# Attention layer of a four-layer graph network: where its value steps, its second softmax and its table loads stand in the order of work

## The chip, the cores and the metric

The kernel runs on one core of one Trainium2 chip. The metric is the device time of one execution in microseconds. The engines are named as the profile names them: PE is TensorE (PEld its weight loads), DVE is VectorE, ACT is ScalarE, POOL is GpSimd, SP is SyncE. [...]

## The reference, cut to what matters

`x` holds 128 graphs of 64 nodes with 256 features each. The kernel keeps it as 64 tiles of 128 partitions (the nodes of two graphs) by 256 features. Four graph layers follow one another, each as a residual with a layer normalisation:

```python
x = _layernorm(x + _L0_gnn_ref(...))   # windows of an LSTM
x = _layernorm(x + _L1_gnn_ref(...))   # two maps with batch norms
x = _layernorm(x + _L2_gnn_ref(...))   # attention over 512 edges
x = _layernorm(x + _L3_gnn_ref(...))   # a spectral layer
```

The change lies in layer 2 and in how layers 1 and 3 meet it:

```python
def _L2_gnn_ref(H, W_lin, W_val, a, W_out, A0, src, dst):
    Xq = (H @ W_lin.T).reshape(bt, n, h, dh)
    Xv = (H @ W_val.T).reshape(bt, n, h, dh)
    e = einsum('behd,hd->beh', leaky_relu(Xq[:, src] + Xq[:, dst], 0.2), a)
    e_t = (e + log(A0[src, dst] + EPS)[None, :, None]).transpose(1, 0, 2)
    ex = exp(e_t - segment_max(e_t, src)[src])
    attn = ex / segment_sum(ex, src)[src]
    Y = segment_sum(attn[..., None] * Vt, src)      # Vt: Xv at dst
    return Y.reshape(bt, n, d) @ W_out.T

def _L3_gnn_ref(features, A, W1, b1, W2, b2):
    # U: eigenvectors of the normalised Laplacian of A
    agg = einsum('mn,bnd->bmd', U.T, features)
    h = relu(agg @ W1 + b1)
    return einsum('nm,bmd->bnd', U, h @ W2 + b2)
```

## The kernel before, in words

**Residual and normalisation.** `X` stays in SBUF through all layers. `Norm` (L1337) adds a product to two tiles of it (`join`, DVE, L1353), takes their statistics (L1362, L1363), and for every n tiles runs one root chain (`inv_sqrt`: DVE L1272, ACT's sqrt L1274, DVE L1275 to L1278, then `ln_sh` L1378) and scales each tile (`X` on ACT, L1383). The root chain and the scaling together are a flush.

**Layer 1's last pass** (`last_pass`, L2048) turns the finished map of layer 1 back, two tiles h at a time, joins them to X and normalises them. `whole(h)` does this for one pair with its own flush; from the pair after that the steps of layer 2 do it themselves.

**Scores** (`scores`, L2227) is a generator of 32 steps, one for two tiles. `follow` (L2145) fixes the order on an engine by hand, and all that it issues is recorded at L2148. Step k expands the products of step k-1 and k to edges (`edges`: 64x512 products `m<-edge_s,xl` and `xh`, whose positive part goes to `xs` on ACT and on DVE), multiplies the next two tiles by both weights (`maps`: `m<-wqv,xT`; the value half is stored to DRAM as `xv`, L2224, from SP's queue except four steps from ACT's), transposes the tiles after these (`transposed`: `m<-ident,X`, then the `xT` copy on DVE) and sums the scores (`products`: `sc<-xs,az`). POOL multiplies `xq` by the attention vector (L2219); DVE sums it, and at the end of each half (16 steps) a linear term `linb` is added to the scores. In the first half of the steps the two pairs `ha` and `hb` of layer 1 are turned and joined as well. Their statistics and the root chain stand partly behind the join (`ha`) and partly in `closed` (`hb`), which runs in the step after; the very last root chain has a place of its own (L2294 to L2296).

**Softmax** (`softmax`, L2303) is a generator of six steps for each half of the scores: shift, exp (L2322), transposes (L2329), sums, a division, and eight indirect DMAs on POOL's queue that scatter the attention values to a DRAM table `attn_d` (L2353). `fetch` (L2358) loads the table of one half back, 4 MB in eight transfers, issued alternately from SP's and POOL's queue, into `M2`.

**Values** (`values`, L2396) is a generator of 33 steps. Step k copies one slice of the table (`load`, `mc` on ACT, L2370), loads `xr` from DRAM (`mapped`, L2376, issued from POOL's queue except four steps from ACT's), multiplies them in 64x64 products (`mixed`, L2390), and copies the result to `yT` (ACT, L2393). It then multiplies the `yT` of step k-1 by the output weights (`ps<-wo,yT`, L2413; called W here) and adds that to tiles 2(k-1) and 2(k-1)+1 of X, with a flush for every four tiles, that is in every second step. Steps 0 to 15 need the first table, steps 16 to 31 the second.

**Layer 3** (`blocks`, L2514) is a generator of 19 steps over 16 blocks of four tiles. Step q does `basis(q)` (products `ps<-bda,X`, L2479, copied to `ag` by ACT, L2481, after which POOL adds `cb` to X, L2483), `first_map(q-1)` (L2489, `h` on DVE, L2492), `back(q-2)` (L2497, `uh` on ACT, L2499) and `second_map(q-3)` (L2507, joined, normalised and stored by SP).

**The order of all this** is written out by hand with `run(...)`, which takes one step of each generator named (L2421 to L2529); within it, a scheduler may still put independent instructions of different steps in another order. Before the change it runs: scores beside layer 1, then scores beside the first softmax, `fetch(0)`, three score steps, seven times a score step and a value step (L2460), and in the last stage the second softmax beside four value steps, then values and layer-3 steps mixed, `fetch(1)`, eight times [value, value, layer 3], two values and the rest of layer 3. There, `basis(q)` for q from 6 on stands behind value step 2q+4.

Of the kernel before, what the change touches and what calls it, by code (L numbers as in the profile page):

```python
# [16 lines left out]
N = 64  # L17
# [4 lines left out]
NT = NB * N // P  # L22
# [1369 lines left out]
def tile_adj_resnorm(ctx: ExitStack, tc: tile.TileContext, I: dict, out: bass.AP, layers: int = 4):  # L1392
    nc = tc.nc
# [653 lines left out]

    def last_pass():  # L2048

        ln = Norm(nc, sy, X, 8, act=True)  # L2050

        def normed(h):
            y = sy.tile([P, 2, 2 * P], F32, tag="y", name="y")
            for c in range(2):
                s.activation(y[:, c, :], Y[h // 2][:, c, h % 2 * 2 * P : (h % 2 + 1) * 2 * P], AF.Identity,
                             bias=sh2[:, c : c + 1], scale=sc2[:, c : c + 1])
            return y

        y = {}

        def turned(h):

            ps, x = pp.tile([P, 512], F32, tag="m", name="m"), y.pop(h)
            for i in range(2):
                for c in range(2):
                    te.transpose(ps[:, i * D + c * P : i * D + (c + 1) * P], x[:, c, i * P : (i + 1) * P], ident)
            ln.join(2 * h, ps, 2)

        def prepare(h):

            if h < 2 * NQ:
                with in_order(s, True):
                    y[h] = normed(h)

        def whole(h):

            with in_order(v, True):
                turned(h)
                ln.stats(2 * h, 2)
            if h == 1:  # L2080
                keep_awake(pp.tile([P, 512], F32, tag="m", name="m"), 2)
            prepare(h + 1)
            with in_order(s, True), in_order(v, True):
                ln.flush()

        prepare(0)
        return ln, turned, prepare, whole
# [10 lines left out]
    with ExitStack() as l2:  # L2098
# [93 lines left out]
        def maps(k, xT, apart=False):  # L2192

            xq, whole, xv = [], sx.tile([P, 2, D], F32, tag="xq", name="xq", bufs=2), sx.tile([P, 2, D], F32, tag="xv", name="xv", bufs=2)
            pss = [pp.tile([P, 512], F32, tag="m", name="m") for _ in range(2)]

            def product(i, cols):
                for c in range(2):
                    follow(te.matmul, pss[i][:, cols], xT[:, i, c, :], wqv[:, c, cols], start=(c == 0), stop=(c == 1))

            def first(i):
                lo, hi = (parts[i][q][:, :: k % 2 + 1][:, :2] for q in range(2))
                x = pss[i][:, :D].rearrange("p (c d) -> p c d", c=2)
                w = whole[:, i, :].rearrange("p (c d) -> p c d", c=2)
                follow(s.copy, hi, x, eng=s)
                follow(s.copy, w, x, eng=s)
                follow(v.tensor_tensor, lo, w, hi.bitcast(F32), ALU.subtract, eng=v)
                xq.append((lo, hi))

            if apart:  # L2210
                for i in range(2):
                    product(i, slice(0, D))
                    first(i)
            for i in range(2):
                product(i, slice(D, 2 * D) if apart else slice(0, 2 * D))
                if not apart:
                    first(i)
                follow(s.copy, xv[:, i, :], pss[i][:, D:], eng=s)
                nc.gpsimd.tensor_tensor(whole[:, i, :], whole[:, i, :], arow, ALU.mult)  # L2219
                yield  # L2220
            sums.append(lambda: follow(
                v.tensor_reduce, lin[:, k // HU, :, :, :, k % HU].rearrange("p c i h -> p i c h"),
                whole.rearrange("p i (c h d) -> p i c h d", c=2, h=2), AX.X, ALU.add, eng=v))
            (s if 22 < k < 27 else nc.sync).dma_start(xvd[k], xv)  # L2224
            yield xq

        def scores():  # L2227


            K = NT // 2  # L2230
            xT = transposed(0)
            *_, xq = maps(0, xT, True)
            whole(2)
            xT = transposed(1)

            def scales(n):

                with in_order(s, True):
                    while n and later:
                        later.pop(0)()  # L2240
                        n -= 1

            held = {}

            def edges(k, c, xq):
                xs, ready = {}, []
                for i in range(2):
                    pl = [pp.tile([P, 512], F32, tag="m", name="m") for _ in range(2)]
                    for part, b in ((0, 0), (0, 1), (1, 0), (1, 1)):
                        r = slice(b * N, (b + 1) * N)  # L2250
                        follow(te.matmul, pl[b], xq[i][part][r, c, :], GGr[r, :], start=(part == 0), stop=(part == 1))
                    for b in range(2):
                        x = xs[b, i] = sx.tile([P, E], F32, tag="xs", name="xs", bufs=8)
                        ready.append(follow(v.tensor_scalar, x, pl[b], 0.0, None, ALU.max, eng=v) if b
                                     else follow(s.activation, x, pl[b], AF.Relu, eng=s))
                held[k, c] = xs, ready

            def closed(n):
                with in_order(v, True):
                    if n:  # L2260
                        ln.stats(2 * n, 2)
                    with in_order(s, True):
                        later.extend(ln.root())

            xl, last = None, None
            for k in range(K):
                ha, hb = (h if h < 2 * NQ else None for h in (2 * k + 3, 2 * k + 4))
                if k:
                    edges(k - 1, 1, xl)
                edges(k, 0, xq)  # L2270
                if hb:
                    prepare(hb)
                if last:
                    closed(last)
                steps = maps(k + 1, xT) if k < K - 1 else iter((None,) * 3)
                next(steps)
                while sums:
                    sums.pop()()
                scales(2)
                next(steps)  # L2280
                scales(2)
                xl, xq = xq, next(steps)
                if k < K - 2:
                    xT = transposed(k + 2)
                if ha:
                    with in_order(v, True), in_order(te, True):
                        turned(ha)
                        if hb:
                            turned(hb)
                        ln.stats(2 * ha, 2)  # L2290
                products([(k - 1, 1), (k, 0)] if k else [(k, 0)], held)
                if hb:
                    prepare(hb + 1)
                elif ha:  # L2294
                    closed(None)
                    scales(2)  # L2296
                last = hb
                if k == K - 1:
                    edges(k, 1, xl)
                    products([(k, 1)], held)  # L2300
                yield

        def softmax(half):  # L2303
# [40 lines left out]
            for c, (eT, rc) in enumerate(zip(eTs, rcs)):  # L2344
                ps = scratch()
                for k in range(4):
# [1 line left out]
                v.tensor_tensor(at[:, :, :, :, c, :].rearrange("p k b u i -> p (k b) i u"),  # L2348
                                eT.rearrange("p k (i u) -> p k i u", u=HU).rearrange("p k (b i) u -> p (k b) i u", b=2),
                                ps.rearrange("p (k i u) -> p k i u", i=4, u=HU), ALU.mult)  # L2350
            for k in range(4):
                for b in range(2):
                    nc.gpsimd.indirect_dma_start(  # L2353
                        out=attn_d[b][:, :], out_offset=bass.IndirectOffsetOnAxis(ap=ix[:, k : k + 1], axis=0),
                        in_=at[:, k, b].rearrange("p u c i -> p (u c i)"), in_offset=None)
# [2 lines left out]
        def fetch(half):  # L2358

            M2[half] = lw.tile([P, N, P], F32, tag="M2", name="M2")  # L2360
            for n0 in range(0, N, 16):
                for b in range(2):
                    (nc.sync, nc.gpsimd)[b].dma_start(
                        M2[half][b * N : (b + 1) * N, n0 : n0 + 16, :],
                        attn_d[b][: N * N, :].rearrange("(d n) q -> d n q", n=N)[:, n0 : n0 + 16, :])

        def load(k):
            half, u_ = divmod(k, HU)
# [6 lines left out]

        def mapped(k):  # L2376
            x = sm.tile([P, 2, D], F32, tag="xr", name="xr", bufs=3)
            (s if 14 < k < 19 else nc.gpsimd).dma_start(x, xvd[k])
            return x

        def mixed(m, x):
# [41 lines left out]
        sc_ = scores()  # L2423
        ln, turned, prepare, whole = last_pass()
        whole(0)
        whole(1)
        run(*[sc_] * (NQ - 1))
        keep1.close()
        lw, sm = own1(valuing, name="l2w", bufs=1), own1(valuing, name="l2s", bufs=2)
# [24 lines left out]
        soft += [softmax(h) for h in range(2)]  # L2454
        run(*[sc_] * (HU - NQ + 1))
        run(*[sc_, soft[0]] * 6)
        fetch(0)
        run(*[sc_] * 3)
        constants()
        run(*[sc_, val] * 7)  # L2460
        scoring.close()
        pp = own1(l2, name="l2m", bufs=2, space=PSUM)

# [3 lines left out]
        with tc.tile_pool(name="l3s", bufs=2) as s3, tc.tile_pool(name="l3p", bufs=6, space=PSUM) as p3:  # L2467
# [55 lines left out]

            l3 = blocks()
            sf = soft[1]
            run(sf, val, sf, val, sf, val, sf, val, sf, l3, l3, val, l3, val)
            fetch(1)
            run(l3, val, l3, val, l3)
            run(*[val, val, l3] * 8, val, val, *[l3] * (NT // 4))  # L2529
        valuing.close()  # L2530


# [60 lines left out]
```

## Time and profile before

| | us |
|---|---|
| three runs, lowest, median, highest | 2227.99, 2230.44, 2233.7 |
| the profiled execution | 2228.17 |
| its span in the profile | 2226.4 |
| busy in the span: PE, DVE, ACT, POOL | 2156.3, 1781.5, 891.8, 206.3 |

The span is the time from the first to the last instruction that the profiler saw, and 1.8 us of the execution lie outside it. PE is busy for 97% of the span; what it misses lies mostly in the last quarter. The page's 40 slices of the span are 55.7 us each; a busy share there says how full an engine is and not what it waits for, so the prediction goes by the waits of PE and by its timeline, and takes durations of single instructions from the groups by form. Two things are to be kept in mind with those rows. A row of the timeline joins neighbouring matmuls of one kind, so its duration is that of the group. And an engine's idle time is put down to the releaser that came last; in brackets behind a row stand the idle time before it and that releaser.

The stages of the span that concern the change are, on PE: layer 1's end at about 1675 us, the scores from there to about 2025 us, and then the last stage.

### The profile page before, as it was taken

The numbers are of one execution on the slowest core, as the hardware profiler recorded it, in microseconds if no ns is written. First come the engines' busy times: TensorE is split into PE (matmuls) and PEld (weight loads), VectorE is DVE, ScalarE is ACT, GpSimd is POOL, SyncE is SP. The second block draws the span as 40 slices with busy tenths as digits, with TensorE's granted clock in tenths as the row PEclk, the third lists the DMA queues.
The fourth block names the chain that finished last, engine by engine and source line by source line (L and its number), as shares of the span: only waits on it lengthen the run. The fifth ranks groups of instructions, "written<-read, shape, count | busy, mean of one in ns | idle before, by whom it ended". The sixth has DMA issues, their size and how long they took to land. (4 is left out here: it accounts for less than half of the span.)

```text
span 2226.4 us, 30062 instructions
## 1 busy us (share of the span) xinstructions
PE 2156.3 (97%) x8828; PEld 1227.0 (55%) x8828; DVE 1781.5 (80%) x9261; ACT 891.8 (40%) x1663; POOL 206.3 (9%) x256
## 2 busy tenths in 40 slices
PE   8999999999999999999999999999998999989897
PEld 6545665445665445665444654554434544447787
DVE  5788887888898899889899899887957886546688
ACT  1432322433332333332333222434436874446575
POOL 0111111101000000000000000000001111313321
PEclk9999999999999999999999999999999999999999
DMA  7001010111010111010111000012210010411522
GB/s 236 22 20 38 1 39 1 38 38 58 1 39 1 39 38 57 1 39 1 38 39 57 1 20 19 8 66 95 76 58 20 29 52 29 114 39 52 144 85 78
DMA packets 44923, 101.55 MB, mean 46 GB/s; under 512 B 5296, under 2 KB 23856, under 8 KB 43472
## 3 DMA queue, kind: packets, MB, share of 16 engines
q1 hardware_dynamic: 37808, 83.59, 10.8%
q0 software_dynamic: 3664, 13.35, 2.2%
q10 hardware_dynamic: 3280, 2.64, 0.5%
q8 instruction: 70, 1.15, 0.2%
q14 instruction: 101, 0.83, 0.1%
HBM read 67.97 MB, written 31.59 MB: 45 GB/s over the span
## 5 line engine op out<-in xcount | busy, mean ns | idle before, releaser
L1756 PE MATMUL pq<-H,wi 128*128 128x512 f32 (+1 forms) x1952 | 780.6, 540 | 1.5 <-ACT gate L1796 1.2
L1796 ACT ACTIVATE gate<-pq,bl 128x512 f32<-128x512 f32 (+1 forms) x504 | 315.5, 632 | 615.0 <-PE pq L1772 501.0
L1756 PEld LDWEIGHTS pq<-H,wi 128*128 128x128 f32 x1952 | 365.5, 190 | 336.8 <-issue 269.7
L1772 PE MATMUL pq<-lh,wh 128*128 128x512 f32 (+1 forms) x1152 | 461.2, 528 | 0.8 <-DVE lh L1814 0.7
L1772 PEld LDWEIGHTS pq<-lh,wh 128*128 128x128 f32 x1152 | 218.4, 190 | 202.4 <-issue 143.5
L1799 ACT ACTIVATE gate<-lc 128x512 f32<-128x512 f32 (+1 forms) x144 | 83.6, 580 | 278.2 <-DVE lc L1811 103.1
L2148 PE MATMUL m<-wqv,xT 128*128 128x512 f32 (+1 forms) x264 | 126.6, 626 | 4.5 <-DVE xT L2148 4.5
L803 POOL PARTITION_ALL_REDUCE qQ<-qSG x62 | 73.8, 1191 | 508.6 <-DVE pc L135 263.6
L2028 PE MATMUL ps<-h,w 128*128 128x512 f32 x256 | 114.5, 604 | 5.0 <-ACT h L2022 2.7
L1383 ACT ACTIVATE X<-X,ln_sh,ln_rs 128x256 f32<-128x256 f32 x187 | 99.1, 593 | 38.8 <-DVE ln_sh L1378 32.4
L1974 PE MATMUL ps<-at,w 128*128 128x512 f32 x256 | 113.1, 593 | 0.0
L2148 DVE TENSOR_SCALAR xs<-m 128x512 f32<-128x512 f32 x128 | 79.6, 677 | 18.5 <-PE m L2148 18.5
L2148 PEld LDWEIGHTS m<-wqv,xT 128*128 128x128 f32 x264 | 51.1, 204 | 66.4 <-issue 49.6
L2148 ACT ACTIVATE xs<-m 128x512 f32<-128x512 f32 x128 | 68.7, 598 | 44.3 <-PE m L2148 43.5
L2028 PEld LDWEIGHTS ps<-h,w 128*128 128x128 f32 x256 | 48.3, 192 | 65.0 <-issue 55.1
L2219 POOL TENSOR_TENSOR xq<-xq,arow 128x256 f32<-128x256 f32 x64 | 46.8, 732 | 377.3 <-DVE xl L2148 377.2
L2148 PE MATMUL m<-edge_s,xl 64*128 64x512 f32 x256 | 68.4, 449 | 13.3 <-ACT xs L2148 11.8
L1974 PEld LDWEIGHTS ps<-at,w 128*128 128x128 f32 x256 | 47.3, 190 | 52.8 <-issue 51.4
L1362 DVE BATCH_NORM_STATS2 ln_st<-X 128x6 f32<-128x256 f32 x192 | 72.9, 415 | 1.3
L2148 DVE TENSOR_TENSOR xl<-xq,xh 128x256 fp32r<-128x256 f32 x64 | 27.3, 426 | 56.6 <-ACT xq L2148 56.6
L131 DVE SCALAR_TENSOR_TENSOR CS<-GA,qE 64x1 f32<-64x1 f32 x294 | 61.8, 210 | 9.5
L131 DVE SCALAR_TENSOR_TENSOR GA<-qtg,CS,GA 64x1 f32<-64x1 f32 x294 | 61.6, 209 | 8.4
(647 smaller groups left out, 3557.5 us busy)
## 6 DMA issues: line engine op xcount, KB each, us to landing
wi<-in_WihT_dram SPq DMA_DIRECT2D x16, 1024.0 KB, 4.9
wh<-in_WhhT_dram SPq DMA_DIRECT2D x12, 1024.0 KB, 6.4
xd<-X SPq DMA_DIRECT2D x16, 512.0 KB, 2.6
X<-xd SPq DMA_DIRECT2D x16, 512.0 KB, 3.4
X<-in_x_dram SPq DMA_DIRECT2D x15, 512.0 KB, 9.0
out_dram<-X SPq DMA_DIRECT2D x15, 512.0 KB, 2.9
xv<-xv SPq DMA_DIRECT2D x28, 256.0 KB, 2.0
xr<-xv POOLq DMA_DIRECT2D x28, 256.0 KB, 2.9
```

The costliest lines, as they stand in the source:

```text
L131: self.nc.vector.scalar_tensor_tensor(o, a, s, b, op0, op1)
L803: gp.partition_all_reduce(S[:, : wide + n], PR[:, : wide + n], N, bass_isa.ReduceOp.add)
L1362: nc.vector.bn_stats(st, self.X[:, k, :])
L1383: nc.scalar.activation(x, x, AF.Identity, bias=sh[:, k : k + 1], scale=rs[:, k : k + 1])
L1756: te.matmul(ps, wi[:, kk, o * P : (o + 1) * P], at(kk, k), start=(kk == 0), stop=(k == 0 and kk == 1))
L1772: te.matmul(ahead[gt, c], wh[:, kk, o * P : (o + 1) * P], hst[:, kk, :M], start=False, stop=(kk == 1))
L1796: s.activation(gates[gt][:, c, :M], ps, AF.Tanh if gt == 2 else AF.Sigmoid, bias=bl[:, p - 1, o : o + 1])
L1799: s.activation(*due.pop())
L1974: te.matmul(ps, w1[:, k, c * P : (c + 1) * P], at[:, k, :], start=(k == 0), stop=(k == 1))
L2028: te.matmul(ys[c], w2[:, k, c * P : (c + 1) * P], h[:, k, :], start=(k == 2), stop=(k == 1))
L2148: ins = make(*a, **k)
L2219: nc.gpsimd.tensor_tensor(whole[:, i, :], whole[:, i, :], arow, ALU.mult)
```

## The change

It does the following:

- Layer 1's last pass takes its small tiles from another pool. `whole` gets a callback that is run behind the join and the statistics and ahead of the flush; `whole(1)` and `whole(2)` use it for the `transposed` of tiles 0 and 1, and `whole(1)` moves into `scores`.
- In `scores` the statistics of both pairs go to `closed` in the step after. The last root chain takes this way too.
- No value step stands beside scores any more: eight score steps follow where seven pairs of a score and a value step stood.
- `fetch` becomes a generator of two portions (the two halves of the partitions, four transfers each), all issued from POOL's queue; the first table's portions alternate with score steps. The scatter runs over the halves first.
- All stores of `xv` and all loads of `xr` are issued from SP's queue.
- The last stage begins with five pairs of a value step and a step of the second softmax, then both portions of the second table. Value and layer-3 steps are then mixed so that `basis(q)` for q from 7 to 15 stands directly behind value step 2q+2.

The number of value steps (33), layer-3 steps (19) and matmuls of each kind stays as it was.

```diff
-        ln = Norm(nc, sy, X, 8, act=True)
+        ln = Norm(nc, sx, X, 8, act=True)
...
-        def whole(h):
+        def whole(h, then=lambda: None):
             with in_order(v, True):
                 turned(h)
                 ln.stats(2 * h, 2)
+            x = then()
             if h == 1:
                 keep_awake(pp.tile([P, 512], F32, tag="m", name="m"), 2)
             prepare(h + 1)
             with in_order(s, True), in_order(v, True):
                 ln.flush()
+            return x
...
-            (s if 22 < k < 27 else nc.sync).dma_start(xvd[k], xv)
+            nc.sync.dma_start(xvd[k], xv)
...
-            xT = transposed(0)
+            xT = whole(1, lambda: transposed(0))
             *_, xq = maps(0, xT, True)
-            whole(2)
-            xT = transposed(1)
+            xT = whole(2, lambda: transposed(1))
...
-            def closed(n):
+            def closed(hs):
                 with in_order(v, True):
-                    if n:
-                        ln.stats(2 * n, 2)
+                    for h in hs:
+                        ln.stats(2 * h, 2)
...
-                        ln.stats(2 * ha, 2)
                 products([(k - 1, 1), (k, 0)] if k else [(k, 0)], held)
                 if hb:
                     prepare(hb + 1)
-                elif ha:
-                    closed(None)
-                    scales(2)
-                last = hb
+                last = [h for h in (ha, hb) if h]
...
-            for k in range(4):
-                for b in range(2):
+            for b in range(2):
+                for k in range(4):
...
-            for n0 in range(0, N, 16):
-                for b in range(2):
-                    (nc.sync, nc.gpsimd)[b].dma_start(
+            for b in range(2):
+                for n0 in range(0, N, 16):
+                    nc.gpsimd.dma_start(
...
+                yield
...
-            (s if 14 < k < 19 else nc.gpsimd).dma_start(x, xvd[k])
+            nc.sync.dma_start(x, xvd[k])
...
-        whole(1)
         run(*[sc_] * (NQ - 1))
...
-        fetch(0)
-        run(*[sc_] * 3)
+        table = fetch(0)
+        run(sc_, table, sc_, table)
         constants()
-        run(*[sc_, val] * 7)
+        run(*[sc_] * 8)
...
-            run(sf, val, sf, val, sf, val, sf, val, sf, l3, l3, val, l3, val)
-            fetch(1)
-            run(l3, val, l3, val, l3)
-            run(*[val, val, l3] * 8, val, val, *[l3] * (NT // 4))
+            run(*[val, sf] * 5)
+            for _ in fetch(1):
+                pass
+            run(val, val, *[l3, val] * 2, *[l3, val, val] * 3, l3)
+            run(*[l3, val, val] * 9, *[l3] * 4)
```

More of the change, by code (lines that the diff above doesn't have):

```diff
@@ L2256, in edges @@
                 held[k, c] = xs, ready
-            def closed(n):
+            def closed(hs):
                 with in_order(v, True):
-                    if n:
-                        ln.stats(2 * n, 2)
+                    for h in hs:
+                        ln.stats(2 * h, 2)
                     with in_order(s, True):
                         later.extend(ln.root())
-            xl, last = None, None
+            xl, last = None, []
             for k in range(K):
```

## The prediction, made before the changed kernel was run

> **What bounds the kernel now.** I read the page's slices first. The tenths of PE are full until the last ten slices (one is 55.7 us), so the change (which touches only the stretch from about 1660 us on) can win only PE's gaps there.
>
> ```profile
> PE   8999999999999999999999999999998999989897
> ```
>
> Then the stretch views. One stretch (1937.4 to 2007.5) holds the scores with value steps between them, the next the steady part of the last stage, the third that stage's start. Columns: length, busy PE, PEld, DVE, ACT, POOL, then PE's clock and the DMA share.
>
> ```profile
> 1937.40:2007.50 70.10, 58.67 (x408) 31.08 (x408) 30.77 (x71) 35.80 (x78) 9.96 (x15) 0.90 0.12 39
> 2101.00:2200.00 99.00, 99.00 (x1034) 88.62 (x1033) 80.70 (x276) 71.43 (x154) 30.96 (x48) 1.00 0.25 80
> 2080.00:2101.00 21.00, 13.12 (x110) 10.53 (x109) 9.63 (x43) 12.61 (x27) 1.14 (x2) 0.76 0.43 123
> ```
>
> The steady part is PE alone: 99.00 of 99.00 us at full clock. The two others lose 11.4 and 7.9 us in waits and more to a clock of 0.90 and 0.76. PE's waits from 1660 us to the end name them:
>
> ```profile
> PE m L2148 <- ACT xs L2148: 11.8, 3, 4.2
> PE ps L2413 <- ACT ag L2481: 5.1, 1, 5.1
> PE m L2148 <- DVE xT L2148: 4.5, 2, 2.3
> PE m L2390 <- ACT mc L2370: 3.0, 1, 3.0
> PE m L2390 <- ACT yT L2393: 2.8, 1, 2.8
> ```
>
> PE's timeline shows what follows a wait (start, duration, idle time before in brackets):
>
> ```profile
> 1837.69 0.50 PE L2148 MATMUL m<-edge_s,xl 64*128 64x512 f32 x2 [3.31 <-ACT xs L2148]
> ...
> 1838.36 5.40 PE L2148 MATMUL m<-wqv,xT 128*128 128x512 f32 x8
> ```
>
> Those 8 products take 3.70 us elsewhere (1914.29). After idle times of 2.2 us and more (2.19, 2.25, 3.31, 4.24, 5.07) PE runs at half rate for some 3.7 us and so loses about 1.85 us; after 1.06, 1.20, 1.61 and 1.69 us it doesn't. [...]
>
> **The change part by part.** Everything is reckoned against the profiled execution: span 2226.4 us, time 2228.17, so 1.8 us outside the span. That execution is 0.1% below the median of the runs (2230.44).
>
> *Start of layer 2.* The xT copy no longer stands behind a root chain on DVE: one wait of 2.25 us and its slow products (1.7) go, while the keep-awake matmuls now stand between. Bounds 0 and 5; I take 3, nearer the sum of 3.9.
>
> *Statistics moved into closed().* A score step with layer-1 normalisation takes 9.47 us (1804.61 to 1814.09), a pure one 8.13 (1912.08 to 1920.21, PE busy throughout). The 1.3 us between them come from a closed loop of DVE and ACT (xs, statistics, root, X, xh, xq, xl, xT, joins). Moving 0.75+0.30 us inside a loop changes its order, not its sum: 0. Bounds: a gain of 7 (half of a join and its aggregations, 0.69+0.30, in each of 15 steps) to a loss of 3 (one instruction of 0.2 us more in each).
>
> *Last root chain.* It goes through an ordinary step instead of standing ahead of the edges: 3.31 + 1.7 = 5.0 gained.
>
> *No value steps beside scores.* Gone: 2.99 and 2 x 4.24 us of waits, 1.4 for the 64x64 matmuls ahead, 3.4 for two slow clocks, 1.3 for three stretched edge groups: 17.6. As a check, 70.1 us of stretch hold 51.9 us at steady durations: 18.2. I take 17.6. The seven value steps' own PE work (2.73 us each: 16 matmul groups 0.90, W 1.83) only moves to the last stage. One thing comes back: after the last score product nothing fills PE between the linear term and the last sc product. Waits of 1.61 and 1.20 become one of about 3.2 with a slow clock: -2.0.
>
> *Table in portions, POOL's queue alone.* xr moves to SP's queue, so POOL's now holds xq's multiplications, scatters, table loads and X+cb. Fetch(0) is needed only some 80 us later (4 MB took about 20 us, 1917.3 to 1939.2). Behind it POOL's xq multiplications feed only the linear term, which is due late. Fetch(1) is issued before the stage's sixth value step and needed at the sixteenth (its first mc): ten value steps (27 us) and seven layer-3 steps of 1.8 to 6.3 us (35) later, some 60 us, against eight scatters of 1.27 us and 20 us of loading: hidden. Cover gone, it would cost what it costs now. The stall of before, whose chain of waits holds the load of M<-attn_d, goes: 5.07 + 1.79 slow + 2.81 + 1.64 slow = 11.3. xv on SP: the xr tile has three buffers and two steps of lead; 0.
>
> Sum of gains: 3 + 0 + 5 + 17.6 - 2 + 11.3 = 34.9.
>
> *The new order of the last stage.* This is the cost. Value step k adds the output of step k-1 to tiles 2(k-1) and 2(k-1)+1 and normalises four tiles in every second step. Layer-3 step q reads tiles 4q to 4q+3 in its first matmuls (basis), so it needs value step 2q+2. Before, step q stood behind value step 2q+4: a whole block (two values, one layer-3 step) lay between. After, from q=7 to q=15, it stands directly behind value step 2q+2. On PE the order of a block is: second_map, W, W, two groups of mixing matmuls, then basis, whose four pairs each wait for ACT's X; then first_map, back. Behind the waiting basis stand, in order, first_map, back, the next second_map and the next W, hence everything.
>
> The chain, with t=0 at second_map's start, and steady durations:
> PE: second_map 0 to 1.83, W to 3.66, W to 5.49, mixing to 7.29.
> DVE: four joins with statistics (0.69 + 0.75 + 0.30), layer 3's root interposed: the last join starts about 5.8; the four layer-2 tiles' is_t is done at 8.9.
> ACT: yT 6.1 to 6.9, mc (1.08) to 7.9, layer 3's X (four, 2.08) 8.45 to 10.5, then the sqrt for layer 2 (0.2), mc to 11.75, and X for layer 2 from 11.75. The first is there at about 12.35.
>
> So PE waits 12.35 - 7.29 = 5.06 us. After such a wait it runs at half rate (1.85 lost, as at 2088.06 below).
>
> ```profile
> 2088.06 3.78 PE L2413 MATMUL ps<-wo,yT 128*128 128x256 f32 x8 [5.07 <-ACT ag L2481]
> ```
>
> These 8 products take 1.99 us in the steady part. The block takes 11.85 us now:
>
> ```profile
> 2134.57 1.95 PE L2479 MATMUL ps<-bda,X 128*128 128x128 f32 x16
> 2136.36 1.95 PE L2489 MATMUL ps<-w,ag 128*128 128x128 f32 x16
> 2138.14 1.06 PE L2497 MATMUL ps<-bdah,h 128*128 128x128 f32 x8
> 2139.03 1.89 PE L2507 MATMUL ps<-w,uh 128*128 128x256 f32 x8
> ...
> 2146.42 0.83 PE L2479 MATMUL ps<-bda,X 128*128 128x128 f32 x6
> ```
>
> It becomes 11.85 + 5.06 + 1.85 = 18.76: 6.91 more. Seven blocks (q=7 to 13): 48.4. At q=14 one mixing group stands before the basis, so 0.90 less of the wait is covered (7.8), at q=15 none (8.7). Sum 64.9.
>
> Its bounds. Below: with empty engines the chain from the end of W to the first X is join, statistics, root and X: 3.19 us from join to X (1965.08 to 1968.27) plus 0.2 and the first X 0.59, together 4.0; mixing covers 1.8, so PE still waits 2.2, 20 us in nine steps, or 22.5 with the longer last two. Without the half rate the middle is 48. Above: everything as worked out.
>
> Net: 34.9 - 64.9 = -30.0. Span 2226.4 + 30.0 = 2256.4, time **2258 us**, 1.3% slower.
>
> **Rivals.**
>
> *The new wait is near its bare length* (2.2 us, the clock not always halved): 34.9 - 22.5 = +12.4, time 2216. For it: DVE and ACT have gaps in the steady part (80.7 and 71.4 of 99 us), and the waits let both run ahead. Against it: ACT's queue in a block puts layer 3's four X and a mc between the value tiles' sqrt and their X. If even this is hidden the gain stands whole: 2193.3. The point that decides is the cost of a block: below 34.9/9 = 3.9 us the kernel becomes faster. 0.17 together.
>
> *Waits as worked out, but no half rate*: 48 instead of 64.9, time 2242. For it: the 64x64 matmuls after the wait of 2.99 were not visibly slower. Against it: the five waits from 2.2 us up, listed above. 0.2.
>
> *The second table is late in spite of its early issue.* It stands on POOL's queue behind scatters and the first X+cb, which needs layer 3's first basis; were it to slip to the seventeenth value step, the 11.3 us come back with the wait: 2269. For it: eight loads stand on one queue where two served before; against it: some 30 us to spare by the sum above. 0.06.
>
> *The change does not do what it says*: the score steps stay at 70 us for 52 us of work because something other than the value steps stalled them. ACT's mc, yT and X do lie between xs in the trace, so it is unlikely: 17.6 less gain, 2276. 0.04.
>
> *Values alone are bound by ACT*: at the start of the last stage five value steps run beside the softmax: ACT needs 0.65 + 1.08 + 1.15 = 2.88 a step against PE's 2.73. A few us, inside the range.
>
> **How the numbers follow.** The forecast 0.5 (2248 to 2266), no half rate 0.2, short waits 0.17, late table 0.06, no gain in scores 0.04, the rest (mixes near no change) 0.03. The range leaves out the short waits and the very end: 2222 to 2276. A difference below 0.3%, 6.7 us, can't be told from none. Faster by more: 0.17. Within: 0.09, from blocks that cost 3.1 to 4.6 us ((34.9 -/+ 6.7)/9), a mix of bare waits and slow clocks. Slower: 0.74.
>
> **What would show it.** In the waits of PE a row of basis (ps) on ACT's X, nine times or, by X tile, more, some 5 us each; PE's clock some 0.8 to 0.9 in the last 170 us instead of 1.00, and blocks of 18.7 us instead of 11.85. The scores end some 20 us earlier for their work, with no wait of 4.24 on xs. No wait of PE on mc, ag or yT near the table. Wrong would be: a basis that waits below 3 us, or a scheduling in which layer 3's X come after those of layer 2; a gain below 25 us ahead of the last blocks; or waits of 5 us with the clock at 1.00.

## The result, and the profile after

| | us |
|---|---|
| before, median (4 runs) | 2229.53 |
| after, median (4 runs, 2259.8 to 2265.01) | 2263.11 |
| ratio after / before | 1.0146 (1.0127 to 1.0165) |
| predicted time and range | 2258.0 (2222 to 2276) |
| after, profiled execution and its span | 2259.8, 2258.0 |

The changed kernel is 1.5% slower. PE's waits from 1660 us to the end, after the change (us in total, times, longest):

```profile
PE ps L2476 <- ACT X L1383: 32.2, 9, 6.0
PE m L2150 <- ACT X L1383: 5.3, 2, 3.4
PE m L2388 <- ACT yT L2391: 4.8, 8, 2.3
PE sc L2150 <- DVE xs L2150: 4.3, 2, 3.2
PE m L2388 <- ACT mc L2368: 3.4, 1, 3.4
...
PE m L2388 <- issue: 2.0, 3, 1.1
```

The first row is new and the largest: basis waits for ACT's X nine times, 32.2 us in all. What led the list before has gone or shrunk: xs on ACT from 11.8 to 0.9 us, xT from 4.5 to 0.2, and ag (5.1) is gone. The other rows are where something else took a place: the transposes at the start of layer 2 now wait for ACT's X (5.3 us, 2.5 before), the mixing waits for yT (4.8 us, 2.8 before, in one piece then), the score steps run out with one wait of 3.2 us, and the first slices of the second table are waited for once.

Five of the late blocks, in the stretch view (length, PE, PEld, DVE, ACT, POOL, clock, DMA share, GB/s):

```profile
2102.40:2192.10 89.70, 68.54 (x641) 62.67 (x641) 40.52 (x165) 46.20 (x96) 14.47 (x20) 0.87 0.18 56
```

Where this stage had PE busy for 99.00 of 99.00 us at a clock of 1.00, PE now misses a quarter of the stretch, and its clock is 0.87. DVE and ACT are below 52%, so no engine is full: they wait for one another. One block on PE's timeline shows how:

```profile
2126.28 1.89 PE L2504 MATMUL ps<-w,uh 128*128 128x256 f32 x8
2128.01 3.62 PE L2411 MATMUL ps<-wo,yT 128*128 128x256 f32 x16
2131.56 0.98 PE L2388 MATMUL m<-mc,xr 64*64 64x64 f32 x32
2132.76 0.97 PE L2388 MATMUL m<-mc,xr 64*64 64x64 f32 x32 [0.23 <-ACT yT L2391]
2137.73 1.22 PE L2476 MATMUL ps<-bda,X 128*128 128x128 f32 x4 [3.99 <-ACT X L1383]
...
2139.17 2.25 PE L2476 MATMUL ps<-bda,X 128*128 128x128 f32 x12
```

It is the order of the prediction: second_map, W, W, mixing, mixing, and then a basis that waits 3.99 us. The two rows of basis hold 16 records in 1.22 + 2.25 us, where the steady part before took 1.95: the half clock (granted 0.59 of full speed from 2137.73 to 2141.42, and 0.50 behind the next such wait, from 2155.17 to 2159.40; 1.00 in the steady part). From basis to basis it is 17.65 us (2120.08 to 2137.73) where it was 11.85; five blocks (2102.44 to 2192.07) take 17.93 on average. Not all nine basis steps wait like this: the waits are 0.29 and 0.77 us at q=7 and q=8, 3.99 or 4.00 at q=9 to 13, then 5.12 and 6.03. At q=7 and 8 the mixing ahead of the basis has already waited, 3.41 us for mc and 2.30 us for yT.

The chain behind the second W, in the same block, on DVE, ACT and PE:

```profile
2133.86 2.08 ACT L1383 ACTIVATE X<-X,ln_sh,ln_rs 128x256 f32<-128x256 f32 x4
2133.88 0.17 DVE L1272 TENSOR_SCALAR is_t<-ln_mv 128x4 f32<-128x4 f32 x1
2135.84 0.20 ACT L1274 ACTIVATE is_s<-is_t 128x4 f32<-128x4 f32 x1
...
2136.88 0.16 DVE L1378 SCALAR_TENSOR_TENSOR ln_sh<-ln_mv,ln_rs 128x4 f32<-128x4 f32 x1
2137.08 2.08 ACT L1383 ACTIVATE X<-X,ln_sh,ln_rs 128x256 f32<-128x256 f32 x4
```

The value tiles' variance (is_t) is ready at 2134.05, but their square root starts at 2135.84: ACT is still scaling layer 3's four tiles, which came 0.02 us earlier. So 1.79 of the 3.99 us stand in ACT's queue; the remaining 2.20 are what the prediction called the bare chain.

### The profile page after: what moved, and what is told of

Its sections match the earlier page's. It is cut to its first block, busy times and chain, and to the rows that moved or that the text cites. A ratio compares the mean times of both kernels' runs of the same rounds, so it can differ in the third digit from the quotient of the medians.

```text
span 2258.0 us, 30107 instructions
## 1 busy us (share of the span) xinstructions
PE 2167.2 (96%) x8828; PEld 1243.6 (55%) x8828; DVE 1776.4 (79%) x9261; ACT 887.5 (39%) x1661; POOL 195.9 (9%) x236
## 5 line engine op out<-in xcount | busy, mean ns | idle before, releaser
L2150 PE MATMUL m<-wqv,xT 128*128 128x512 f32 (+1 forms) x264 | 118.6, 592 | 0.8 <-DVE is_t L1272 0.7
L1383 ACT ACTIVATE X<-X,ln_sh,ln_rs 128x256 f32<-128x256 f32 x187 | 99.1, 595 | 31.4 <-DVE ln_sh L1378 21.7
L2028 PEld LDWEIGHTS ps<-h,w 128*128 128x128 f32 x256 | 48.3, 192 | 65.0 <-issue 55.1
L2476 PE MATMUL ps<-bda,X 128*128 128x128 f32 x256 | 47.8, 356 | 32.2 <-ACT X L1383 32.2
```

The source lines that it names most:

```text
L1383: nc.scalar.activation(x, x, AF.Identity, bias=sh[:, k : k + 1], scale=rs[:, k : k + 1])
L2028: te.matmul(ys[c], w2[:, k, c * P : (c + 1) * P], h[:, k, :], start=(k == 2), stop=(k == 1))
L2150: ins = make(*a, **k)
L2476: te.matmul(ps[:, j * P : (j + 1) * P], X[:, q * 4 + j, k * P : (k + 1) * P], bdu, start=True, stop=True)
```

## The experiments

The theory is that the whole loss comes from the missing distance between the flush of a value step and the basis that reads its tiles, that the other parts of the change gain, and that the loss of a block is a wait (bare chain plus ACT's queue) plus the half clock behind it. The rivals were that the last stage is slow for another part of the change, that the half clock costs nothing of its own, and that ACT's queue is only idle time.

### The distance given back

```diff
-            run(*[l3, val, val] * 9, *[l3] * 4)
+            run(*[val, val, l3] * 9, *[l3] * 4)
```

> The changed kernel, with only its last line of the order of work altered: from block q=6 on, a layer-3 step stands behind value step 2q+4 again, as before the change. Theory (the missing distance between a flush and the basis that reads its tiles is the whole loss, some 61 us by the trace after): no waits of basis on ACT's X, blocks of 11.85 us, 2263 - 61 = about 2202 us, 1.2% faster than before. Rival (the last stage is slow for another part of the change, its queues or its data): blocks stay well above 12 us and the time stays above 2230 us.

2204.96 us (2200.8 to 2207.76), 0.989 (0.987 to 0.991) of before. In the stretch view and on PE's timeline of this run:

```profile
2090.00:2180.00 90.00, 90.00 (x929) 80.89 (x929) 74.10 (x253) 63.54 (x137) 23.41 (x34) 1.00 0.24 76
```

```profile
2134.34 1.95 PE L2476 MATMUL ps<-bda,X 128*128 128x128 f32 x16
...
2146.19 1.95 PE L2476 MATMUL ps<-bda,X 128*128 128x128 f32 x16
```

PE is full again at full clock, a block takes 11.85 us, and no row of basis stands among the waits. One line of the order is worth 2263.1 - 2205.0 = 58.1 us, and all else in the change, taken together, gains. This is the fastest version here: it beats both kernels.

### The missing distance in the kernel before

```diff
-            run(*[val, val, l3] * 8, val, val, *[l3] * (NT // 4))
+            run(*[l3, val, val] * 9, *[l3] * 4)
```

> The kernel before, with only the new order of the end: layer-3 step q directly behind value step 2q+2 from q=6 on. Theory: the same nine waits of some 4 us and half clock, 2229 + 61 = about 2290 us. Rival (the waits need another part of the change, such as all xr loads on SP's queue): stays within 10 us of 2229 us.

2292.62 us, 1.0271 (1.0247 to 1.0296) of before, so 63.9 us more, where some 61 were expected. PE's timeline has the same waits (3.99, 5.12 and 6.03 after the change), without any other part of the change:

```profile
2097.51 3.78 PE L2479 MATMUL ps<-bda,X 128*128 128x128 f32 x16 [11.16 <-ACT X L1383]
...
2188.88 1.23 PE L2479 MATMUL ps<-bda,X 128*128 128x128 f32 x4 [3.99 <-ACT X L1383]
...
2243.41 3.98 PE L2479 MATMUL ps<-bda,X 128*128 128x128 f32 x16 [5.13 <-ACT X L1383]
...
2262.43 3.98 PE L2479 MATMUL ps<-bda,X 128*128 128x128 f32 x16 [6.03 <-ACT X L1383]
```

The last two are the steps q=14 and 15, with one and with no mixing group in front: some 1 us more each time, as the prediction had it. Ten steps wait here and not nine, 48.3 us in all, and the first, q=6, for another reason: ACT's X stands behind a mc that waits 12.28 us for the second table, which is late here as it was before the change (there it cost waits of 5.07 and 2.81 us). The other nine wait 37.1 us, against 32.2 after the change. The rival of another part of the change falls.

### A distance of one value step

```diff
-            run(*[l3, val, val] * 9, *[l3] * 4)
+            run(val, *[l3, val, val] * 8, l3, val, *[l3] * 4)
```

> The changed kernel, with one value step between the flush and the basis that reads its tiles, where it has none and before had a whole block. PE then has one W and about one and a half mixing groups, 3.1 us, behind the flushing W, instead of 1.8 us. Theory (a chain of some 6.0 us behind W, of which 2 us are ACT's queue): waits of 2.2 to 2.9 us with half clock in part of them, some 32 us lost in nine blocks, about 2234 us. Rival (only the bare chain of 4.0 us counts): waits below 1 us, no half clock, about 2207 us.

2241.62 us, 1.0055 (1.0038 to 1.0072) of before: 7 us above the theory's number and far from the rival's. On PE's timeline:

```profile
2136.97 0.71 PE L2476 MATMUL ps<-bda,X 128*128 128x128 f32 x4 [2.44 <-ACT X L1383]
...
2151.34 0.71 PE L2476 MATMUL ps<-bda,X 128*128 128x128 f32 x4 [2.45 <-ACT X L1383]
...
2165.70 0.71 PE L2476 MATMUL ps<-bda,X 128*128 128x128 f32 x4 [2.44 <-ACT X L1383]
...
2166.47 2.70 PE L2476 MATMUL ps<-bda,X 128*128 128x128 f32 x12
...
2181.72 0.71 PE L2476 MATMUL ps<-bda,X 128*128 128x128 f32 x4 [2.47 <-ACT X L1383]
```

From q=9 to 14 the waits (2.44 to 2.80 us) lie within the expected 2.2 to 2.9. The block is 14.37 us (2136.97 to 2151.34) where the clock stays full (1.50 us for the twelve basis products) and 16.02 (2165.70 to 2181.72) where it does not (2.70 us), after the same wait. What the forecast missed lies outside these blocks: a wait of 3.4 us for mc near the table's change (as after), and 5.75 us at q=15, where no value step is left to put in between.

### ACT's queue emptied

```diff
-                    ln3.add(q * 4 + j, ps, 2, 2 if q == NT // 4 - 2 else 0)
                     t = q * 4 + j + 2
+                    if j and 3 <= q <= 12:
+                        ln3.join(t - 2, ps, 2)
+                        ln3.stats(t - 2, 2)
+                        ln3.root()
+                    else:
+                        ln3.add(t - 2, ps, 2, 2 if q == NT // 4 - 2 else 0)
```

> The changed kernel without the scaling of layer 3's tiles on ACT (four activations) in the blocks 3 to 12: its output lacks that last scaling there. In the trace after, the square root of the value tiles' flush stands 1.79 us behind these activations on ACT's queue. Theory (the wait of 4.0 us is the bare chain of 2.2 us plus these 1.8): waits of basis on X of about 2.2 us, the half clock in part of them, 2263 - 9 x 1.8 - some 8 = about 2239 us. Rival (DVE or the bare chain ends last, ACT's queue is idle time): waits stay near 4 us and the time at 2263 us.

2248.48 us (2242.57 to 2254.82), 1.0102 (1.0081 to 1.0123) of before: 15 us less than the changed kernel, where 24 were expected. Its profile is that of its fastest execution. In one block of it, on ACT, DVE and PE, and below in a later block on PE:

```profile
2105.65 2.05 ACT L2368 COPY mc<-M 128x512 f32<-128x512 f32 x2
...
2106.65 0.17 DVE L1272 TENSOR_SCALAR is_t<-ln_mv 128x4 f32<-128x4 f32 x1
2107.59 0.22 ACT L1274 ACTIVATE is_s<-is_t 128x4 f32<-128x4 f32 x1
...
2109.50 0.71 PE L2476 MATMUL ps<-bda,X 128*128 128x128 f32 x4 [2.98 <-ACT X L1383]
...
2176.81 1.23 PE L2476 MATMUL ps<-bda,X 128*128 128x128 f32 x4 [2.25 <-ACT X L1383]
```

The second mc copy moved into the place of the scaling, so the square root still starts 0.77 us behind is_t (2106.82) instead of 1.79. The queue's part fell by 1.02 us and PE's wait by 1.01 (3.99 to 2.98): what stands in ACT's queue there is paid by PE one to one. In the later block no mc got between: is_t is done at 2174.87, the square root starts at 2174.91, and PE waits 2.25 us, the bare chain alone. The mechanism holds; that the whole 1.8 us would come free in every block was wrong.

### The wait filled with unused products

```diff
+                if 7 <= q:
+                    ps = bank()
+                    for _ in range(5):
+                        te.matmul(ps[:8, :], ln.mv.rearrange("p k c -> p (k c)"),
+                                  wo.rearrange("p c d -> p (c d)"), start=True, stop=True)
                 ag[q] = s3.tile([P, 2, 512], F32, tag="ag", name="ag")
```

> The changed kernel with five products that nobody uses ahead of each basis from q=7 on (128x512 moving columns, about 2.3 us; they read the flush's statistics, so that they come in the wait and not ahead of it). The idle stretch of 4 us becomes one of about 1.5 us, while the data come no earlier. Theory (of the 5.8 us lost a block some 1.6 are the halved clock behind the wait): block 17.65 becomes about 16.1 us, nine times, about 2249 us, the clock in the last 170 us near 1.00. Rival (the half clock costs nothing that the waits don't cost anyhow): 2263 us or more.

2258.22 us, 1.0129 (1.0112 to 1.0146) of before, 5 us less than the changed kernel. Inconclusive by its size: the five products took 4.46 us (0.89 each, twice the assumed; the profile lists two records for each) and ended at 2144.11 in a block whose first X was there at 2142.95. So a second run with three (`range(3)`):

> As the run with five unused products ahead of each basis, with three. Each took 0.89 us and not the 0.46 assumed, so the five lasted 4.46 us and ended 1.05 us behind the data. Theory (half clock costs some 1.6 us a block): three last 2.7 us, basis starts with the data, block about 16.0 us, 2258 - 9 x 1.05 = about 2249 us. Rival (the clock is not what was gained): 2258 to 2263 us.

2241.47 us, 1.0062 (1.0045 to 1.0079) of before, some 7.5 us below the number expected: the run with five had also lost 10.2 us ahead of the basis of q=7 (2090.99 there, 2080.79 here). In this run's stretch and on its timeline:

```profile
2102.40:2192.10 89.70, 81.76 (x759) 62.68 (x757) 47.75 (x190) 48.16 (x101) 14.35 (x21) 1.00 0.18 57
```

```profile
2132.17 0.71 PE L2481 MATMUL ps<-bda,X 128*128 128x128 f32 x4 [1.70 <-ACT X L1383]
...
2148.19 0.71 PE L2481 MATMUL ps<-bda,X 128*128 128x128 f32 x4 [1.10 <-ACT X L1383]
```

The same stretch has a clock of 1.00 instead of 0.87, and three blocks take 16.02 us as expected (the one ahead of them 17.43), against 17.93 on average. From second_map to basis it is 11.45 us in both kernels (2136.74 to 2148.19 here, 2126.28 to 2137.73 there), so the data come no earlier, and what is gone is the half clock behind the wait. Work that nobody uses makes the kernel faster, so the half clock has a price of its own: 1.9 us in a block of 16.02. From the basis of q=7 to the end the two profiles differ by 15.0 us (174.3 and 159.3), 1.7 for each of the nine steps. Another 2.9 us lie ahead, where this run lacks the waits of mixing on "issue" and most of the one on mc. The medians differ by 21.6 and not by these 17.9, since the profile of the changed kernel is that of its fastest execution.

### The value steps beside the scores

```diff
-            run(*[val, sf] * 5)
-            for _ in fetch(1):
-                pass
-            run(val, val, *[l3, val] * 2, *[l3, val, val] * 3, l3)
-            run(*[l3, val, val] * 9, *[l3] * 4)
+            run(sf, val, sf, val, sf, val, sf, val, sf)
+            for _ in fetch(1):
+                pass
+            run(l3, l3, val, l3, val, l3, val, l3, val, l3)
+            run(*[val, val, l3] * 8, val, val, *[l3] * (NT // 4))
...
-        run(*[sc_] * 8)
+        run(*[sc_, val] * 7, sc_)
```

> The run with the distance given back, and beside that seven value steps beside the scores as before the change, the last stage in the order of before (the second table fetched right behind the softmax). Theory (value steps beside scores cost 17.6 us, and spare 2.0 at the end of the scores): 2205 + 15.6 = about 2220 us, with waits of 3 to 4 us on xs and mc between the scores. Rival (the score steps stall for something else, or the stall is paid elsewhere without them): about 2205 us.

2233.86 us, 1.002 (1.001 to 1.003) of before. The waits of 4.24 us on xs are back, but a row stands ahead of them that was not expected:

```profile
1938.17 1.61 PE L2388 MATMUL m<-mc,xr 64*64 64x64 f32 x32 [13.69 <-ACT mc L2368]
```

The first value step waits 13.69 us for the first table: it began one score step earlier than before the change, and the portions were issued between score steps. So the run mixed two things, and a second one kept them apart:

```diff
-        run(sc_, table, sc_, table)
-        constants()
-        run(*[sc_, val] * 7, sc_)
+        run(table, table, sc_, sc_, sc_)
+        constants()
+        run(*[sc_, val] * 7)
```

> As the run with value steps beside scores, which began them one score step too early for the first table (a wait of 13.7 us on mc came in between). Here both portions of the first table are issued at once and three score steps lie ahead of the first value step, as before the change. Theory (value steps beside scores cost 15.6 us net, the 13.7 us were the table alone): about 2220 us. Rival (they cost what the run before gave, 29 us): about 2234 us.

2216.9 us, 0.9948 (0.9932 to 0.9965) of before. That is 11.9 us more than the 2205.0 without value steps there; 15.6 were forecast. The run differs in the last stage too, which has the order of before. Marks on the two timelines keep these apart (1839.77, 2021.72 and 2214.7 here, 1838.61, 1986.28 and 2202.2 there, for the first linear term, the end of the last score products and the end of the span). Less the moved work of 16.4 us (seven mixing groups, five and a half W), the scores take 17.9 us more with value steps between them, and the last stage 6.6 us less. The fetch by portions is hidden in the changed kernel: its first value step comes only at 1986.24.

### The second table alone

```diff
-            run(sf, val, sf, val, sf, val, sf, val, sf, l3, l3, val, l3, val)
-            fetch(1)
-            run(l3, val, l3, val, l3)
+            run(sf, val, sf, val, sf, val, sf, val, sf)
+            fetch(1)
+            run(l3, l3, val, l3, val, l3, val, l3, val, l3)
```

> The kernel before, with only the load of the second table moved ahead of the first two layer-3 steps, right behind the softmax; both queues as before. Theory (11.3 us are lost to the late table): no wait of PE on ag and yT near it, 2229 - 11 = about 2218 us. Rival (the scatter and loads on POOL's queue still stand behind its additions, and the table is late anyhow): 2229 us.

2230.14 us, 1.0001 (0.9992 to 1.0011) of before: nothing moved. POOL's timeline shows why (M is the load of the table):

```profile
2049.16 4.83 POOL L2483 TENSOR_TENSOR X<-X,cb 128x256 f32<-128x256 f32 x7
...
2071.50 2.15 POOL L2363 DMA_DIRECT2D M<-attn_d  x4 [6.12 <-issue]
```

The scatters still stood behind layer 3's additions on POOL's queue, and POOL's half of the load behind the scatters. It starts 46.0 us behind the last score products (2025.46); before it is 45.9 (2069.01 and 2023.11). The line that issues the load was not what set its time. A second run keeps the first additions behind the scatters:

```diff
-                for j in range(4):
-                    nc.gpsimd.tensor_tensor(X[:, q * 4 + j, :], X[:, q * 4 + j, :], cb, ALU.add)
+                with in_order(nc.gpsimd, q < 3):
+                    for j in range(4):
+                        nc.gpsimd.tensor_tensor(X[:, q * 4 + j, :], X[:, q * 4 + j, :], cb, ALU.add)
```

> As the run with the second table's load moved in the kernel before, which moved nothing: POOL's queue still held the scatters behind its additions of cb. Here those additions are kept behind the scatters. In the trace of before the scatters are spread from 2044 to 2062 us, bare they take 10 us, so the table lands some 8 to 9 us earlier. Theory (the late table costs 11.3 us): 2229 - 9 = about 2220 us, the wait on ag gone or below 2 us. Rival (the table is bound by the transfers' bandwidth or PE loses the time elsewhere): 2229 us.

2221.23 us, 0.9963 (0.9949 to 0.9977) of before: 7.2 us gained, and the wait on ag is gone. POOL's loads in it:

```profile
2064.33 2.15 POOL L2363 DMA_DIRECT2D M<-attn_d  x4
```

That is 35.9 us behind the last score products (2028.39), 10 us earlier than in the run before: the last scatter stands 5.9 us earlier, and the pause from it to the load is 4.2 us shorter, which no row explains. This profile is that of the slowest of five executions (2226.36). From its last score products to its end it takes 196.2 us, before it was 203.3 (2023.11 to 2226.4), so the 7.1 us between them do lie in this stage.

## Why the prediction was right, and where it was not

**The loss, 64.9 us forecast, 58.1 measured** (the changed kernel less the one with its distance given back). Mechanism, place and order were right: no engine at its bound, a basis that waits for ACT's X, the half clock behind it, the last two waits longer. But only seven of the nine basis steps wait so. At q=7 and q=8 the same blocks lose their time earlier, to mc and yT, and are no shorter for it (18.73 us from q=7 to q=8, 17.64 to q=9). The wait was taken as 5.06 us and is 3.99 at q=9 to 13. With t=0 at second_map's start (2126.28) the last join stands at 5.8 as worked out, but layer 3's root chain is done at 7.4, so its X start on ACT at 7.6 and not at 8.45; behind them the square root comes at 9.6 and the value tiles' X at 10.8 instead of 11.75. Mixing ends at 7.45 instead of 7.29. The sum for DVE was too long, for the value tiles as well (is_t is done at 7.8 and not at 8.9), but that one is off the path, since the square root stands in ACT's queue until 9.6. The half clock was taken as 1.85 us a block; filled with other work, a block of 16.02 gains 1.9, and the nine gain 15.0.

**The bare chain of 2.2 us** as the lower bound was right: 3.99 less the 1.79 of ACT's queue is 2.20, and the run without layer 3's scaling shows that the queue's part is paid in full and, in one block with the queue free, a wait of 2.25.

**The rule "half rate after 2.2 us and more"**, read from one trace, fails both ways. In the run with one value step of distance the same wait of 2.44 us was followed by the half clock in some blocks (2.39 and 2.70 us for twelve basis products) and not in others (1.50 us). After the change the last sc products follow a wait of 3.17 us at full rate (1.06 us for eight), in the run with the distance given back the same wait is followed by 1.93 us. And in the second run on the table a wait of 1.63 us is followed by the half clock (1.77 us for eight sc products from 2018.28 on), where the kernel before runs the same products in 1.07 us after 1.61.

**The gains, 34.9 us forecast, 24.5 measured** (2229.5 less 2205.0). The prediction named a gain below 25 us ahead of the last blocks as a sign of being wrong, and by half a microsecond it is one. The marks that follow are on PE's timelines of before and of the run with the distance given back, whose spans are 2226.4 and 2202.2 us, each counted from the end of layer 1 (1673.70 and 1674.25). The start of layer 2 gained 2.7 (3 forecast; the wqv products at 1712.49 and 1710.35). From there to the first linear term (1845.12 and 1838.61) 4.4 were gained (5 for the last root chain, 0 for the statistics; no run takes these two apart). From there to the end of the last score products (2024.17 and 1986.28) 31.4 are gone, of which 16.4 are the moved work of value steps: 15.0 gained, 15.6 forecast. So 22.1 of 23.6 came as forecast up to there, and the run that puts the value steps back gives 17.9 for the last of them.

**The term that failed is the table's, 11.3 us.** Taken alone, an earlier table gave 7.2. In the changed kernel with its distance given back only 2.7 us are left for the whole last stage. The stall of before is gone, but in its place come losses that were not forecast (this is PE's timeline of that run):

```profile
1984.35 1.93 PE L2150 MATMUL sc<-xs,az 128*32 128x512 f32 x8 [3.17 <-DVE xs L2150]
1986.21 3.21 PE L2388 MATMUL m<-mc,xr 64*64 64x64 f32 x64
1989.35 3.78 PE L2411 MATMUL ps<-wo,yT 128*128 128x256 f32 x8
...
2015.43 0.34 PE L2388 MATMUL m<-mc,xr 64*64 64x64 f32 x3 [0.95 <-issue]
2016.14 0.26 PE L2388 MATMUL m<-mc,xr 64*64 64x64 f32 x1 [0.37 <-issue]
2016.87 0.75 PE L2388 MATMUL m<-mc,xr 64*64 64x64 f32 x17 [0.46 <-issue]
2017.55 3.58 PE L2411 MATMUL ps<-wo,yT 128*128 128x256 f32 x8
...
2036.00 0.98 PE L2388 MATMUL m<-mc,xr 64*64 64x64 f32 x32 [1.18 <-ACT yT L2391]
```

At half rate behind the scores some 3.3 us are lost (3.21 instead of 1.88, 3.78 instead of 1.99, and a little in the next mixing), then 1.78 on "issue", 1.6 of half rate behind it (3.58 instead of 1.99), 1.18 on yT and 0.71 on mc (2076.74). That is 8.6 of the 11.3. The prediction had one slow clock at the end of the scores; here the half rate lasts into the value steps, and in the profile of the changed kernel it is missing there altogether. The statement that no wait of PE on mc or yT would remain near the table also failed: the change has one of 3.41 us on mc, since the first mc of the second table stands behind X on ACT (2077.09 to 2079.07), though the table is there (its loads were issued by 2024.1, and none took more than 21.6 us).

So the total came closer than its parts: 24.5 - 58.1 = -33.6 us, where 34.9 - 64.9 = -30.0 were forecast. The gains were 10.4 us too large and the loss 6.8, and these cancel in part, which is luck.

## What to carry to other kernels

When two generators are interleaved by hand, count how many steps lie between the step that finishes a tile and the step that reads it; here, at distance zero, 4 us of join, statistics, square root and scaling stood open on PE in a block, and the half clock behind them (1.9 us of a block), with DVE and ACT half idle. Look at what a scaling engine has in its queue between a statistic and its use: 1.02 us less there made the wait 1.01 us shorter. And ask which instruction on which queue sets a transfer's time before moving the line that issues it.

## What the runs showed of the hardware

In these runs the length of one idle stretch did not decide alone whether the half clock followed it. In the run with one value step of distance it followed 2.44 us in two blocks (2.39 and 2.70 us for twelve basis products) and did not follow 2.44 and 2.45 us in two others (1.50 us). It followed 3.17 us in the run with the distance given back and not in the changed kernel (1.93 and 1.06 us for eight sc products), and 1.63 us in the second run on the table while it did not follow 1.61 us in the kernel before (1.77 and 1.07 us). What else decides, no run shows.

The waits on "issue" at the start of the last stage stand in five profiles: 2.0 us in the changed kernel, 1.8 with the distance given back, 1.7 with a distance of one value step, 1.9 with five unused products, and 1.9 in the second run on the table (1.1 of mixing, 0.8 of W). In the other seven there are none. In the changed kernel they lie between 2011.4 and 2013.9, and POOL issues six scatters one behind another at some 1.3 us from 2005.36 to 2012.8; in the second run on the table they lie between 2054.0 and 2058.0, and six such scatters go from 2049.29 to 2056.7. In the kernel before and in the first run on the table at most three follow one another so closely there. But the first table's scatters in the kernel before, six at the same pace from 1905.23 on, have no such wait of PE beside them. No run changes the scatters alone, so what causes the waits stays open.
